# The bias matmul of a graph layer: 128 rows of the array in place of 6

## The chip, the cores and the metric

The kernel runs on one NeuronCore of a Trainium2 chip. A core has a matrix engine (TensorE, in the profile PE, with its weight loads shown apart as PEld), a vector engine (VectorE, DVE), a scalar engine (ScalarE, ACT), GpSimd (POOL) and SyncE (SP), which here only issues transfers. Each engine runs its own instructions in order, and semaphores hold the order between engines. Data come from main memory through 16 DMA engines into the on-chip memory of 128 partitions; TensorE writes its results to a second, smaller memory, PSUM.

The metric is the device time of one launch in microseconds: the median of three runs.

## What is computed

Input x has 32 batches of 512 x 1024 fp32 values, adj is a 512 x 512 matrix. Two layers follow each other, each with a residual and a normalisation over the last axis:

```python
# layer 0: attention over the 1024 nodes
q = einsum('c,bcn->bn', wq, x);  k = einsum('c,bcn->bn', wk, x)
scores = leaky(q[:, None, :] + k[:, :, None])        # slope 0.01
att = softmax(scores, axis=-1)
agg = einsum('bcn,bmn->bcm', x, att)
x = layernorm(x + relu(einsum('oc,bcm->bom', adj, agg) + bm[None, :, None]))
# layer 1
W = adj * adj
x = layernorm(x + einsum('bnf,nm->bmf', x, W) + bias)
```

The bias of layer 1 has 1024 values, one for each column; every row of the 512 x 1024 result of a batch gets the same bias row added. This addition is what the change touches.

## The kernel before, in words

One core works through the 32 batches, several of them in flight at once. A batch passes these stages; the short names are those of the program's functions.

- `load` brings x in (four transfers of 512 KB). `parts` makes the two score vectors on TensorE, with stationary operands of 32 columns (line 220); `cols`, `row_out` and `row` turn and spread them.
- `product` multiplies x by adj, 32 fp32 matmuls a batch (line 311), `product_copy` takes them out of PSUM on ScalarE.
- The softmax isn't formed. The nodes are ranked by score (`rank` on VectorE, `count` on ScalarE), their rows scattered to memory in that order by GpSimd (`scatter`, line 325), loaded back (`sums_load`), summed from both ends (`up`, `down`, and the `carry` matmuls of line 381), and written as a table (`table_write`). For each node `gather` (line 433, GpSimd) fetches the row at its place, and `mix_scale` and `mix` (lines 455 and 460) weigh its two halves.
- `turn` transposes the mixed rows on TensorE (line 484), `residual` adds bm, applies relu and adds x on VectorE (line 492), `spread0`, `root0` and `norm0` normalise.
- Layer 1 is a 512 x 512 by 512 x 1024 product, done in the Winograd form of a 2 x 2 block product with seven smaller products. VectorE forms T1 to T4 from the quarters of x; TensorE runs U, V, Y, C11, Z, C12 and C21 for each of two row groups g. Several of these accumulate in the same PSUM tile: U, V, Y and C21 in `sum_ps`, C11, Z and C12 in `pair_ps`. `quarter` (line 537) runs one such product: two fp32 matmuls of 128 x 128 by 128 x 512, each of which the profile shows as two records.
- ScalarE and VectorE put the parts together (`U_copy`, `V_copy`, `Z_copy`, `upper`, `lower_left`, `lower_right`), `spread1`, `root1` and `norm1` normalise, `store` writes out.

The bias enters inside `quarter`. U starts the `sum_ps` tile, Z starts its half of the `pair_ps` tile, and each does so with one more matmul ahead of the fp32 ones: line 540, `matmul(ps, first, bias_p, start=True, stop=False)`. `bias_p` is the moving operand, 6 rows of 512 bf16 values: each half of the bias row as a sum of three bf16 parts, so that nearly all of fp32 is kept, with signs and sums such that one set of rows serves both U and Z. `first` is the stationary operand, a column of 6 values repeated 128 times by a step of zero: `first_0` for U, `first_10` (all ones) for Z. There are 2 x 2 bias matmuls a batch, 128 in all. Both operands are made once, in `bias_parts` (line 177), which runs in the head of the program, on VectorE.

All work is put in order by hand: a long list of words such as `U.-8.0 ct.-5.4 rk.-5.5` names function, batch (relative) and index, one list for the head, one for the steady loop and one for the tail. `emit` (line 659) calls the functions in that order. Each engine runs its own instructions in the order in which they were emitted. In the steady loop the order on TensorE is, for a batch: transposes, the score matmuls of a later batch, transposes, products, carry, products, U, C11, Z, V, Y, C12, C21, products, carry.

Buffers that matter: x has four buffers, so the load of a batch starts when the C12 matmuls of the batch four before are over; the gathered rows (`got`), the table (`tab`) and the products (`zt`) have one each. PSUM has four half-size tiles (products, scores, carry, `sum_ps`) and two full-size tiles (transposes and `pair_ps`).

Of the kernel before, what the change touches and what calls it, by code (L numbers as in the profile page):

```python
# [35 lines left out]
BF16 = mybir.dt.bfloat16  # L36
# [6 lines left out]
P = 128  # L43
# [6 lines left out]
def adj_resnorm_kernel(  # L50
# [10 lines left out]
    nc = tc.nc  # L61
# [3 lines left out]
    H = 512  # L65
# [4 lines left out]
    const = ctx.enter_context(tc.tile_pool(name="const", bufs=1))  # L70
# [30 lines left out]
    own, spare = small[0:6, 9:14], small[0:1, 14:15]  # L101
# [44 lines left out]
    A11, A12 = adj_2[:, 0:2, 0:Q], adj_2[:, 2:4, 0:Q]  # L146
    S1, minus_A22 = adj_2[:, 0:2, Q:C], adj_2[:, 2:4, Q:C]
    S2, S3, S4 = [const.tile([P, 2, Q], F32, name=f"S{i}") for i in (2, 3, 4)]
    bias_p = const.tile([6, H], BF16, name="bias_p")
    first = const.tile([6, 16], BF16, name="first")  # L150
    first_0, first_10 = first[:, 0:1].broadcast_to([6, P]), first[:, 1:2].broadcast_to([6, P])

    def weights():
        t = p1.tile([P, C], F32, tag="m", name="rows_tp")[:, 0 : 3 * CT]
# [22 lines left out]
    def bias_parts(b):  # L177


        i6 = ident[0:6, 0:6]  # L180
        nc.vector.tensor_tensor(own[:, 0:3], i6[:, 0:3], i6[:, 3:6], ALU.subtract)
        nc.vector.tensor_reduce(own[:, 3:4], i6[:, 3:6], axis=AX.X, op=ALU.add)
        nc.vector.tensor_scalar(own[:, 4:5], own[:, 3:4], -1.0, None, ALU.mult)
        nc.vector.tensor_copy(first[:, 0:1], own[:, 4:5])
        nc.vector.memset(first[:, 1:2], 1.0)
        rest, done = room[:, 0, :], room[:, 1, :]
        for i in range(3):
            part = one.tile([P, H], BF16, tag="junk_s", name=f"bias_part_{i}")[0:6, :]
            nc.vector.tensor_copy(part, rest)
            if i < 2:  # L190
                nc.vector.tensor_tensor(rest, rest, part, ALU.subtract)
            if i == 0:
                nc.vector.tensor_scalar(done, part, own[:, 0:1], None, ALU.mult)
            else:
                nc.vector.scalar_tensor_tensor(
                    done, part, own[:, i : i + 1], done, ALU.mult, ALU.add
                )
        nc.vector.tensor_copy(bias_p, done)

    def apart(group, ins):  # L200

# [435 lines left out]
    def store(b, m):  # L637
# [14 lines left out]
        "11": C11, "12": C12, "21": C21, "Uc": U_copy, "Vc": V_copy, "Zc": Z_copy, "up": upper,  # L652
        "lr": lower_right, "ll": lower_left, "ls": lower_sum, "s1": spread1, "r1": root1,
        "n": norm1, "st": store, "bias": bias_parts,
    }
    pool_ops = ("sc", "g", "r1")
# [306 lines left out]
```

## Time and profile before

| | |
|---|---|
| time of the runs, median of 3 (lowest, highest) | 2055.75 us (2049.65, 2059.41) |
| span of the profiled execution, first to last instruction | 2048.6 us |
| TensorE busy | 1978.8 us (97%), 6353 matmul records |
| weight loads busy | 931.7 us (45%) |
| VectorE busy | 1671.6 us (82%) |
| ScalarE busy | 1491.4 us (73%) |
| GpSimd busy | 864.3 us (42%) |
| traffic | 557.93 MB, mean 272 GB/s |
| mean granted TensorE clock | 0.989 |

The profile gives no time of its own for the profiled execution besides its span. The largest groups on TensorE are the products (line 311, 899.8 us in 2048 records), the seven products of layer 1 (lines 542 and 577), and the transposes (line 484, 131.7 us in 1024 records). In a profile line "128*128" is the size of the stationary operand, rows by columns; what follows is the moving operand or, for weight loads, what is loaded. The number before the bar is busy time in microseconds and the mean of one in nanoseconds; after the bar stands the idle time of the engine just before these instructions and what ended it. "issue" means that nothing in the profile was being waited for. Ends of matmuls are modelled, so their durations overlap; starts are read instead.

### The profile page before, as it was taken

To read this page: it belongs to the slowest core of one execution; us is meant where nothing else is said; L and a number is where in the kernel's file an instruction comes from. 1 tells how busy PE (TensorE), PEld (TensorE's weight loads), DVE (VectorE), ACT (ScalarE), POOL (GpSimd) and SP (SyncE) were. 2 spreads that over 40 slices of the span, in tenths; PEclk is the share of its full clock that TensorE was granted. 3 is DMA by queue.
4 is the path that set the end of the run, shared out by engine and by line. 5 is a ranking of instruction groups with operands and counts; after the bars stand their busy time and mean duration, and the time that the engine had idled before them with its cause. 6 is when DMAs were issued, how large, how long until landed. Compare 5 with 4: busy or idle time off the path is not lost. (4 is left out here: it accounts for less than half of the span.)

```text
span 2048.6 us, 21657 instructions
## 1 busy us (share of the span) xinstructions
PE 1978.8 (97%) x6353; PEld 931.7 (45%) x6353; DVE 1671.6 (82%) x2746; ACT 1491.4 (73%) x2560; POOL 864.3 (42%) x1114
## 2 busy tenths in 40 slices
PE   8999899999999999999999999999999999999876
PEld 4444444444444444444444444444444444444332
DVE  7888887889788888888889888889888888788673
ACT  3567777788677778777777877777877777777566
POOL 5334542544444443443343444343443454444431
PEclk9999999999999999999999999999999999999998
DMA  6758667867678767677867777866777866677752
GB/s 220 283 204 335 257 271 294 314 258 282 237 281 326 297 261 286 268 282 305 313 259 282 274 281 295 323 256 272 283 275 295 329 260 256 247 287 285 273 206 82
DMA packets 142830, 557.93 MB, mean 272 GB/s; under 512 B 15044, under 2 KB 15184, under 8 KB 134520
## 3 DMA queue, kind: packets, MB, share of 16 engines
q1 hardware_dynamic: 85328, 354.38, 44.5%
q0 software_dynamic: 57344, 202.15, 25.6%
q8 instruction: 50, 0.82, 0.2%
q14 instruction: 68, 0.56, 0.1%
q10 hardware_dynamic: 40, 0.02, 0.0%
HBM read 287.07 MB, written 269.42 MB: 272 GB/s over the span
## 5 line engine op out<-in xcount | busy, mean ns | idle before, releaser
L311 PE MATMUL z_ps<-adj_t,x 128*128 128x512 f32 x2048 | 899.8, 593 | 0.0
L311 PEld LDWEIGHTS z_ps<-adj_t,x 128*128 128x128 f32 x2048 | 386.3, 190 | 459.9 <-issue 451.6
L325 POOL DMA_INDIRECT sorted_z<-zt,to x256 | 354.7, 1386 | 450.6 <-ACT zt L317 379.1
L433 POOL DMA_INDIRECT got<-table,of x256 | 278.7, 1089 | 227.1 <-issue 77.7
L272 DVE SCALAR_TENSOR_TENSOR junk_v<-qb,qkc,tie 128x1024 uint8<-128x1024 f32 x256 | 327.9, 1281 | 4.1
L285 ACT ACTIVATE junk_s<-qb,qkc 128x1024 uint8<-128x1024 f32 x256 | 294.4, 1150 | 11.4 <-DVE of L292 5.4
L477 POOL TENSOR_SCALAR tv<-tv 128x1 f32<-128x1 f32 x128 | 41.9, 328 | 469.7 <-ACT junk L470 466.4
L455 ACT ACTIVATE got<-got,w 128x512 f32<-128x512 f32 x256 | 173.2, 714 | 71.6 <-DVE w L450 70.4
L317 ACT COPY zt<-z_ps 128x512 f32<-128x512 f32 x256 | 145.4, 579 | 76.8 <-PE z_ps L311 76.5
L460 DVE SCALAR_TENSOR_TENSOR got<-got,w 128x512 f32<-128x512 f32 x256 | 184.1, 745 | 6.4 <-ACT got L455 5.4
L492 DVE SCALAR_TENSOR_TENSOR x<-agg_ps,small,x 128x1024 f32<-128x1024 f32 x128 | 161.6, 1280 | 18.4 <-PE agg_ps L484 18.0
L373 DVE SCALAR_TENSOR_TENSOR tab<-tab,ac 128x513 f32<-128x513 f32 x224 | 167.7, 748 | 2.1
L597 DVE SCALAR_TENSOR_TENSOR g<-pair_ps,g 128x1024 f32<-128x1024 f32 x64 | 78.2, 1221 | 106.3 <-PE pair_ps L542 100.6
L633 ACT ACTIVATE g<-g,nb,tv 128x1024 f32<-128x1024 f32 x128 | 157.6, 1238 | 5.8 <-POOL nb L627 5.8
L470 ACT ACTIVATE junk<-g,tv 128x1024 uint8<-128x1024 f32 x128 | 146.7, 1146 | 20.7 <-DVE g L597 18.0
L470 ACT ACTIVATE junk<-x,tv 128x1024 uint8<-128x1024 f32 x128 | 147.1, 1149 | 15.6 <-DVE x L492 12.8
L406 DVE TENSOR_TENSOR tab<-tab,carry 128x2052 f32<-128x2052 f32 x64 | 145.0, 2292 | 7.3 <-ACT carry L388 6.6
L363 DVE SCALAR_TENSOR_TENSOR tab<-tab,ac 128x514 f32<-128x514 f32 x192 | 144.1, 750 | 7.4 <-ACT ac L349 5.9
L542 PE MATMUL sum_ps<-x,adj 128*128 128x512 f32 x256 | 130.2, 632 | 16.2 <-ACT x L510 16.2
L484 PE MATMUL agg_ps<-ident,got 128*128 128x128 f32 x1024 | 131.7, 279 | 8.9 <-DVE got L460 3.7
L510 ACT ACTIVATE x<-x,tv 128x1024 f32<-128x1024 f32 x128 | 138.3, 1148 | 1.7 <-DVE tv L506 1.7
L484 PEld LDWEIGHTS agg_ps<-ident,got 128*128 128x128 f32 x1024 | 115.9, 143 | 35.2 <-issue 11.6
(118 smaller groups left out, 2597.7 us busy)
## 6 DMA issues: line engine op xcount, KB each, us to landing
table<-tab SPq DMA_DIRECT2D x64, 2056.0 KB
tab<-sorted_z SPq DMA_DIRECT2D x64, 1028.0 KB
x<-in_x_dram SPq DMA_DIRECT2D x128, 512.0 KB
out_dram<-g SPq DMA_DIRECT2D x128, 512.0 KB
qb<-q_row SPq DMA_DIRECT2D x32, 512.0 KB
sorted_z<-zt,to POOLq DMA_INDIRECT x256, 3.7
got<-table,of POOLq DMA_INDIRECT x256, 8.6
adj_in<-in_adj_dram SPq DMA_DIRECT2D x1, 1024.0 KB
```

Source lines behind the costliest of these rows:

```text
L272: nc.vector.scalar_tensor_tensor(junk, s.qb, s.q[:, j : j + 1], tie[:, at : at + N], ALU.subtract, ALU.is_gt, accum_out=s.rank[:, j : j + 1],)
L285: nc.scalar.activation(junk, s.qb, AF.Sign, bias=s.k[:, j : j + 1], accum_out=s.sign[:, j : j + 1])
L311: nc.tensor.matmul(s.z[j], xt[:, c, j * P : (j + 1) * P], adj_t[:, c, :], start=(c == 0), stop=(c == CT - 1),)
L325: nc.gpsimd.indirect_dma_start(out=sorted_z[b % 2][:, :], out_offset=bass.IndirectOffsetOnAxis(ap=s.to[:, j : j + 1], axis=0), in_=zt[:, j ...
L373: nc.vector.scalar_tensor_tensor(v, v, c, s.zs[:, j + 1, 0:D], ALU.mult, ALU.add)
L433: nc.gpsimd.indirect_dma_start(out=s.got[:, j, :], out_offset=None, in_=table[b % 2][:, :], in_offset=bass.IndirectOffsetOnAxis(ap=s.of[:, ...
L455: nc.scalar.activation(down, down, AF.Copy, scale=s.w[:, 1, j : j + 1])
L460: nc.vector.scalar_tensor_tensor(up, up, s.w[:, 0, j : j + 1], down, ALU.mult, ALU.add)
L470: nc.scalar.activation(junk, t, AF.Square, bias=v[0][:, i : i + 1], scale=-float(N), accum_out=v[1][:, i : i + 1],)
L484: nc.tensor.transpose(s.agg[o][:, j * P : (j + 1) * P], s.got[:, j, o * P : (o + 1) * P], ident)
L492: nc.vector.scalar_tensor_tensor(t[:, o, :], s.agg[o], nbm[:, o : o + 1], t[:, o, :], ALU.max, ALU.add, accum_out=s.v0[0][:, o : o + 1],)
L633: nc.scalar.activation(g, g, AF.Identity, bias=s.nb[:, m : m + 1], scale=s.v1[1][:, m : m + 1])
```

## The change

The two operands of the bias matmul get 128 rows. Both tiles are set to zero once, and the six rows of values are then written into rows 0 to 5 as before. The matmul on line 540 keeps its text; its operands are now 128 x 128 and 128 x 512 in place of 6 x 128 and 6 x 512. The added rows contribute zeros to the sum.

```diff
-    bias_p = const.tile([6, H], BF16, name="bias_p")
-    first = const.tile([6, 16], BF16, name="first")
-    first_0, first_10 = first[:, 0:1].broadcast_to([6, P]), first[:, 1:2].broadcast_to([6, P])
+    bias_p = const.tile([P, H], BF16, name="bias_p")
+    first = const.tile([P, 16], BF16, name="first")
+    first_0, first_10 = first[:, 0:1].broadcast_to([P, P]), first[:, 1:2].broadcast_to([P, P])
+    nc.vector.memset(bias_p, 0.0)
+    nc.vector.memset(first, 0.0)
...
-        nc.vector.tensor_copy(first[:, 0:1], own[:, 4:5])
-        nc.vector.memset(first[:, 1:2], 1.0)
+        nc.vector.tensor_copy(first[0:6, 0:1], own[:, 4:5])
+        nc.vector.memset(first[0:6, 1:2], 1.0)
...
-        nc.vector.tensor_copy(bias_p, done)
+        nc.vector.tensor_copy(bias_p[0:6, :], done)
```

## The prediction

> **What bounds the kernel now.** I read the page's busy shares first, then busy time by stretch, then the groups of the changed line with shapes kept apart, and last the order in time around one bias matmul.
>
> Busy time by stretch (first the length, then the time and count of each engine, the granted clock, the DMA share, GB/s):
>
> ```profile
> 740.00:1040.00 300.00, 300.00 (x972) 141.60 (x972) 252.69 (x418) 227.75 (x394) 125.40 (x167) 1.00 0.73 286
> 1040.00:1340.00 300.00, 300.00 (x933) 140.65 (x932) 252.79 (x418) 227.69 (x391) 126.55 (x165) 1.00 0.74 287
> ...
> 1900.00:2048.60 148.60, 108.92 (x307) 48.68 (x305) 80.28 (x128) 90.43 (x140) 45.76 (x71) 0.91 0.51 193
> ```
>
> In the middle TensorE (first engine column) has no idle microsecond, at full clock; VectorE has 16% free, ScalarE 24%. So a microsecond taken from TensorE there is a microsecond of the kernel until another chain comes due. In the last 149 us TensorE idles 40.
>
> The changed line, by form (busy us, mean ns | idle before it):
>
> ```profile
> L540 PE MATMUL sum_ps<-bias_p,first 6*128 6x512 bf16 x64 | 24.6, 385 | 1.1 <-ACT zt L317 1.1
> L540 PE MATMUL pair_ps<-bias_p,first 6*128 6x512 bf16 x64 | 24.6, 385 | 0.0
> L540 PEld LDWEIGHTS <-first 6*128 6x128 bf16 x128 | 11.7, 91 | 96.7 <-issue 96.7
> ```
>
> The 385 ns has a modelled end and is no price. The telling figure is the last: the weight path stands idle 96.7 / 128 = 0.76 us before each load of `first`, with nothing to wait for. Before an ordinary load it is 0.24 us.
>
> Matmuls in order of time (start, us, ...), then weight loads:
>
> ```profile
> 1002.24 0.38 PE L540 MATMUL pair_ps<-bias_p,first 6*128 6x512 bf16 x1
> 1002.55 1.98 PE L542 MATMUL pair_ps<-x,adj 128*128 128x512 f32 x4
> 1004.47 0.38 PE L540 MATMUL pair_ps<-bias_p,first 6*128 6x512 bf16 x1
> ...
> 1010.04 1.88 PE L542 MATMUL sum_ps<-zt,S 128*128 128x512 f32 x4
> 1011.75 1.88 PE L542 MATMUL pair_ps<-x,S 128*128 128x512 f32 x4
> 1013.47 1.88 PE L542 MATMUL sum_ps<-zt,S 128*128 128x512 f32 x4
> ```
>
> ```profile
> 1001.28 0.19 PEld L577 LDWEIGHTS pair_ps<-x,adj 128*128 128x128 f32 x1 [0.24 <-issue]
> 1002.23 0.09 PEld L540 LDWEIGHTS <-first 6*128 6x128 bf16 x1 [0.76 <-issue]
> 1002.55 0.30 PEld L542 LDWEIGHTS pair_ps<-x,adj 128*128 128x128 f32 x2 [0.23 <-DVE junk_v L272]
> ```
>
> Four fp32 records take 1013.47 - 1011.75 = 1.72 us (1.715 over several), and each holds two passes of 512 columns: 0.214 us a pass. With a bias matmul ahead, the same four take 1004.47 - 1002.24 = 2.23 us. So one bias matmul costs 0.515 us, although it is one pass of 512 columns: **0.30 us of it is bubble**. An ordinary load starts while the matmul before runs, so the matmul follows at once. The load of `first` starts at 1002.23, 0.09 after the last fp32 pass streamed out (1001.71 + 0.43), and its matmul starts with it; the next fp32 load again starts only after the bias matmul. 0.09 pause + 0.09 load + 0.215 pass + 0.02 + 0.11 load = 0.52: both loads around it are exposed.
>
> [...] The trace agrees as far as it can: it has one other change of tile, fp32 to fp32 with no change of type, the 32-column matmuls of the scores, with the same mark before and an exposed load after:
>
> ```profile
> 62.94 0.19 PEld L311 LDWEIGHTS z_ps<-adj_t,x 128*128 128x128 f32 x1 [0.24 <-issue]
> 63.89 1.45 PEld L220 LDWEIGHTS qk_ps<-x,wqk 128*32 128x32 f32 x32 [0.76 <-issue]
> 65.76 0.73 PEld L381 LDWEIGHTS carry_ps_True<-end,before 128*128 128x128 f32 x4 [0.41 <-issue]
> ```
>
> Again 0.76. From plain matmuls to transposes, full tile to full tile, there is no gap (carry at 1034.07, four records of 0.215, transposes at 1034.94). What the trace lacks is bf16 on a full tile: whether the type alone breaks the overlap isn't shown. [...] here 6 rows took 91 ns and an exposed 128-row load 0.11 us, near enough.
>
> **The change, part by part.**
>
> Two memsets. 512 bf16 columns at the rate of the `tie` memset (1.66 us for 1920) are 0.44 us, 16 columns 0.06 as the small memsets. They stand on VectorE after the `zero` memset (ends 3.91), ahead of the copy at 7.20, which waits 3.29 us for TensorE. Cost 0; without that cover, 0.5 us once. Nothing else waits on them: the first bias matmul is at 133.3. The two copies and the small memset into rows 0 to 5 have their old sizes: 0. SyncE and GpSimd get nothing new.
>
> The 128 matmuls: one pass of 512 columns stays, on 128 rows. Lower bound of its cost: fully overlapped, 0.214, a saving of 0.30 each, at most 38.5 us in all. Nothing lets it go lower. Upper bound: the bubble stays and the load takes 0.19 (the duration of overlapped 128-row fp32 loads) in place of 0.09: 0.10 worse each. I take full overlap, because an exposed load comes with a change of tile everywhere I looked and never without one.
>
> Where the saving counts (bias matmuls by stretch): 3 before 140 us, 18 in 140 to 440, 95 in 440 to 1900, 9 in 1900 to 2007, 3 after. The chain of waits runs from 1896 to 2008 outside TensorE (sorting, table, gathers, mixing, residual); TensorE even waits 11.6 us for ScalarE at 1971. So those 9 count nothing; the last 3 are on the chain. 119 x 0.301 = 35.8 us.
>
> Deductions. In 140 to 440 TensorE waits 14.8 us in all (4.6 and 3.2 for ScalarE's copy, 2.6 for a T3, smaller ones), released partly by things that don't move with it. I let 8 of the 18 fall into those: 2.4 us.
>
> In the steady loop (61.06 us a batch) the U pair of bias matmuls comes ahead of the copies that release the last scatters; from there, scatter, eight gathers, their landing, and mixing run beside TensorE to the transposes, and the Z pair lies alongside. So the U pair's 0.6 us moves both paths, the Z pair's 0.6 us only TensorE's. How much room is there? Mixing against transposes, an ordinary batch and a tight one:
>
> ```profile
> 1092.75 2.21 DVE L460 SCALAR_TENSOR_TENSOR got<-got,w 128x512 f32<-128x512 f32 x3
> 1096.18 1.91 PE L484 MATMUL agg_ps<-ident,got 128*128 128x128 f32 x16
> ```
>
> ```profile
> 1032.94 2.21 DVE L460 SCALAR_TENSOR_TENSOR got<-got,w 128x512 f32<-128x512 f32 x3
> 1034.94 1.91 PE L484 MATMUL agg_ps<-ident,got 128*128 128x128 f32 x16
> ```
>
> The last mix serves the fourth transpose, 0.33 us after the first: room 1.55 us in the ordinary batch, 0.12 in the tight one. Of eight batches from 668 to 1096 two are tight, six have 1.4 to 2.0. One batch in five, say, of some 25, loses 0.5 us: 2.5 us. Next late after that is the gathers' landing, since the load of x starts when C12 ends, so earlier, and shares the DMA engines (74% busy) with them; the ordinary batch has 1 us left for it. Between transposes and U no bias matmul lies, so the norm that U waits for (ends 1053.83, U at 1055.57) isn't pressed.
>
> Sum: 35.8 - 2.4 - 2.5 = **30.9 us saved**. The profiled span of 2048.6 becomes 2017.7. For that execution only its span is given; the median of the runs lies 7.15 above it, the lowest 1.05. I keep that distance: 2055.75 - 30.9 = **2025 us**.
>
> **The rivals.**
>
> The type, not the tile, breaks the overlap: fp32 to bf16 and back costs what it costs on any number of rows. For it: every bias matmul changes both at once. Against: the 0.76 mark of the scores, where the type stays. Time 2056, no change. Chance 0.12.
>
> Half: one of the two exposed loads is cured, say that of `first`, not the fp32 one after. About half of 31: 2040. Chance 0.07.
>
> Slower: the bubble stays for the type's sake and the load, in the open ahead of each bias matmul, takes 0.19 over 128 rows where 6 took 0.09. 119 x 0.10 = 11.9 us: 2068. It passes 0.5% from 0.086 us a matmul (10.3 / 119). Against: the exposed 128-row load at 1002.55 took 0.11 before its matmul. Chance 0.05.
>
> That the matmul stays a small tile (trailing zeros cut away) is excluded: it is given 128 rows, and the score matmuls' tile follows their operand's width.
>
> **How the numbers follow.** Full overlap 0.76, with a range of its own: 2013 (all 38.5 and the runs' spread of 4) to 2037 (12 more microseconds lost to gathers and ties). The half case reaches to 2047. Together these leave out the no-change and slower cases, 0.17, and a few hundredths of edge: 2013 to 2047. 0.5% (10.3 us) is about what a measurement of this kernel can tell from no change. Faster 0.76 + 0.07 = 0.83, same 0.12, slower 0.05.
>
> **What would show it.** Right: bias matmul shown as 128*128, idle before its load near 0.24 us, start of bias matmul to start of the next 1.93 us in place of 2.23, batch period near 60 us, and short waits of transposes on VectorE's mix in the tight batches. Wrong: 0.76 still there with 128*128 (the type did it); 2.23 gone but the period still 61 (the gathers have taken over).

## The result, and the profile after

The changed kernel takes 2054.66 us (median of 20 runs, 2049.41 to 2062.92) beside 2054.91 for the kernel before (20 runs, 2047.89 to 2059.41): ratio 1.0004, 95% interval 0.9994 to 1.0013. The change does nothing to the time that can be measured; 31 us fewer were forecast. The profiled execution has a span of 2048.0 us beside 2048.6.

And yet the change did on TensorE just what it was to do. The line of the bias matmul by form, in the changed kernel (its line numbers are 2 higher than before; the kernels of the experiments have their own):

```profile
L542 PE MATMUL pair_ps<-bias_p,first 128*128 128x512 bf16 x60 | 22.7, 379 | 0.0
L542 PEld LDWEIGHTS <-first 128*128 128x128 bf16 x128 | 12.6, 99 | 30.5 <-issue 30.5
```

The idle time of the weight path before a load of `first` is 30.5 / 128 = 0.24 us in place of 0.76, the mark of an ordinary load. (60 records in place of 64: some matmul records are missing from this trace.) The same stretch of one batch, in order of time:

```profile
1000.79 0.38 PE L542 MATMUL pair_ps<-bias_p,first 128*128 128x512 bf16 x1
1001.00 1.88 PE L544 MATMUL pair_ps<-x,adj 128*128 128x512 f32 x4
1002.72 0.38 PE L542 MATMUL pair_ps<-bias_p,first 128*128 128x512 bf16 x1
```

From bias matmul to bias matmul it is 1002.72 - 1000.79 = 1.93 us in place of 2.23: the bubble of 0.30 is gone, all of it. To the start of the next matmul the bias matmul now takes 0.21 us, half of the 0.43 us of an fp32 record ((1002.72 - 1001.00) / 4), so that a record counts as two such passes, as in the forecast. TensorE's own work of a batch falls from 61.03 us to 61.03 - 4 x 0.30 = 59.83. But now TensorE has idle time in the middle, where it had none, in the view by stretch:

```profile
740.00:1040.00 300.00, 298.41 (x976) 143.97 (x980) 253.51 (x419) 229.54 (x396) 128.16 (x167) 1.00 0.74 287
1040.00:1340.00 300.00, 297.85 (x951) 143.60 (x958) 254.22 (x420) 230.18 (x396) 128.82 (x167) 1.00 0.74 287
```

The first column after the length is TensorE: 298.41 and 297.85 of 300 where before both stretches were full. (Since ends of matmuls are modelled, small lags inside a run of matmuls still show as busy, so the loss is larger than these 2 us.) In the view of waits TensorE waits for one thing in the loop (740 to 1640 us), and VectorE is held up longer than before by the landing of the gathered rows. Engine and line, what it waited for, us in total, times, longest; first the changed kernel's TensorE and VectorE:

```profile
PE carry_ps_True L383 <- ACT zt L319: 5.4, 8, 1.3
...
DVE w L448 <- DMA got<-table,of: 70.0, 30, 3.7
```

then VectorE in the kernel before, where TensorE had no wait at all in these 900 us:

```profile
DVE w L446 <- DMA got<-table,of: 43.6, 24, 3.2
```

VectorE waits 70 us in place of 44 for the landing, in 30 batch halves in place of 24; its wait for TensorE fell meanwhile (line 599, 56.1 us, for 74.0). What TensorE gained reappears as a wait for a transfer.

Where in the program the time is given back, read from the starts of the score matmuls (us from the span's start):

| | score matmul of batch 8 | batch 25 | batch 31 | end of span |
|---|---|---|---|---|
| before | 420.5 | 1464.6 | 1834.4 | 2048.6 |
| changed | 423.7 | 1462.4 | 1833.9 | 2048.0 |

From batch 8 to 25, 17 periods, 17 x 1.20 = 20.4 us could be had; 1044.1 - 1038.7 = 5.4 came. The mean period of batches 10 to 23 is 60.81 us beside 61.09; single batches of the changed kernel have 60.0 to 61.8. Ahead of that, between batches 7 and 8, the changed kernel has one period of 68.9 us where it was 63.1, and near the end, between batches 28 and 29, one of 66.6 where it was 61.9. (The score matmuls run three batches ahead of layer 1, so the first is the passage of layer 1 from batch 4 to 5.) These two places alone cost 10.5 us, more than the gain of the loop; the period after the second of them gives 1.2 back (57.2 for 58.4).

The granted clock is no cause in the loop: there it is 1.00 in both kernels, and a kernel below with a mean clock of 0.985, beside 0.984 for the changed one, is 29 us faster. At the passage from batch 4 to 5 it has a part. After a wait of 6.64 us four matmul records of C21 run at half clock and take 3.58 us, where the kernel before, at full clock, takes 1.82 (the changed kernel first; the third number from the end is the clock):

```profile
401.82:405.40 3.58, 3.58 (x5) 1.52 (x5) 3.48 (x10) 0.00 (x0) 0.00 (x0) 0.50 1.04 412
```

```profile
400.54:402.36 1.82, 1.82 (x4) 0.86 (x5) 1.82 (x4) 0.00 (x0) 0.00 (x0) 1.00 1.04 407
```

That is 1.8 us of the 5.8 lost there. From 1900 us to the end the mean clock is 0.88 beside 0.91; what this costs is not separated.

**The second loop.** Followed from batch to batch, the work outside the bias matmuls forms a ring of its own: carry matmuls, transposes, scores, products, the carry downwards, its copy on ScalarE, the table's last sums on VectorE, ranks and T1 to T3, the gathers on GpSimd, their landing, the weights of the mixing, the mixing on ScalarE, with product copies queued behind it, and with them a free PSUM tile for the next carry. The chain of waits of the changed kernel shows it (start, length, engine, what):

```profile
804.94 0.38 ACT carry L390
...
820.97 1.98 POOL got L435
...
831.08 13.20 DMA got<-table,of
...
850.53 0.48 ACT zt L319
851.05 0.70 PE carry_ps_True L383 x2
```

In this turn of the ring, from one carry to the next, the landing is the longest piece, 13.20 us. No bias matmul lies on this ring. How the end of it looks in one batch (its U starts at 993.49), in order of time on all engines:

```profile
1026.93 0.17 DVE L448 TENSOR_TENSOR w<-bd,got 128x8 f32<-128x8 f32 x1 [3.16 <-DMA got<-table,of]
...
1027.75 0.72 ACT L457 ACTIVATE got<-got,w 128x512 f32<-128x512 f32 x1 [1.77 <-DVE w L452]
...
1032.96 1.53 ACT L319 COPY zt<-z_ps 128x512 f32<-128x512 f32 x3
1033.58 0.70 PE L383 MATMUL carry_ps_True<-end,before 128*128 128x257 f32 x2 [0.86 <-ACT zt L319]
```

The last gathered rows land 33.4 us after U (read, here and below, from the start of their weighing on VectorE). ScalarE has waited 1.77 us for the weights; its last mixing ends at 1033.06, the product copies stand behind it, and the second half of the carry waits 0.86 us for them. The carry of the same batch in the kernel before runs without a gap:

```profile
1034.07 1.03 PE L381 MATMUL carry_ps_True<-end,before 128*128 128x257 f32 x4
```

In 12 of batches 10 to 23 the changed kernel starts the second half of the carry 0.05 us after such a copy ends, so the copy holds it; in the kernel before this is so in one.

**Why the landing is late.** The load of x (2.1 MB) starts as soon as the C12 matmuls have ended, and so moves with TensorE: 22.80 us after U before, 21.70 now (medians of batches 10 to 23). The first gather, though, starts 9.27 us after U before and 9.36 now. So the load moved 1.1 us into the gathers. From 15 us after U to the landing of the gathered rows, with the sorted rows, the gathered ones and x under way, the DMA share stays above 1. The kernel before, by stretches of 3 us (U at 1055.57; the last two columns are the DMA share and GB/s):

```profile
1070.57:1073.57 3.00, 3.00 (x9) 1.32 (x8) 0.00 (x0) 3.00 (x7) 2.22 (x3) 1.00 1.03 409
...
1085.57:1088.57 3.00, 3.00 (x9) 1.33 (x8) 1.07 (x7) 1.54 (x3) 2.01 (x6) 1.00 1.02 408
1088.57:1091.57 3.00, 3.00 (x9) 1.33 (x8) 3.00 (x7) 3.00 (x6) 0.32 (x1) 1.00 0.18 70
```

For six such stretches in a row the rate is 400 to 414 GB/s at a share of 1.02 to 1.04; in the next 3 us it is 70, and after that nothing is moved. The mean share of 0.74 over 300 us hides this. (The view counts a packet's bytes and time where it starts, so that a share can pass 1, and single stretches elsewhere read higher, 443 GB/s at 1.05 from 1058.57 us; what the engines could move at most, no run shows.) That the stretch is full is the author's estimate from its share. If it is full, x can only come earlier at the cost of the gathered rows: their last landing moved from 31.95 to 32.80 us after U, 0.85 later, while TensorE's carry is due 1.10 us earlier (38.63 us after U for 39.73). That the one comes of the other is for the experiments to show.

### The profile page after: what moved, and what is told of

It reads as the page before. It is cut to its first block, busy times and chain, and to the rows that moved or that the text cites. A ratio compares the mean times of both kernels' runs of the same rounds, so it can differ in the third digit from the quotient of the medians.

```text
span 2048.0 us, 21627 instructions
## 1 busy us (share of the span) xinstructions
PE 1956.9 (96%) x6321; PEld 945.1 (46%) x6353; DVE 1670.9 (82%) x2748; ACT 1491.8 (73%) x2560; POOL 874.5 (43%) x1114
## 4 chain that ended last, share of the span: by engine, by line
PE 45%; DMA 16%; DVE 11%; POOL 8%; ACT 5%; issue 5%; SPq 0%; DVEq 0%; ACTq 0%; POOLq 0%
PE z_ps L313 20%; DMA got<-table,of 12%; PE sum_ps L544 9%; POOL got L435 6%; PE agg_ps L486 4%; PE pair_ps L544 4%; DVE tab L408 3%; DVE junk_v L274 3%; PE pair_ps L579 3%; PE qk_ps L222 2%; DMA sorted_z<-zt,to 2%; ACT junk L472 2%; POOL sorted_z L327 1%; DVE got L462 1%; ACT got L457 1%
## 5 line engine op out<-in xcount | busy, mean ns | idle before, releaser
L327 POOL DMA_INDIRECT sorted_z<-zt,to x256 | 367.6, 1436 | 436.1 <-ACT zt L319 367.8
L479 POOL TENSOR_SCALAR tv<-tv 128x1 f32<-128x1 f32 x128 | 46.7, 365 | 470.1 <-ACT junk L472 466.8
## 6 DMA issues: line engine op xcount, KB each, us to landing
table<-tab SPq DMA_DIRECT2D x64, 2056.0 KB
```

The source lines that it names most:

```text
L327: nc.gpsimd.indirect_dma_start(out=sorted_z[b % 2][:, :], out_offset=bass.IndirectOffsetOnAxis(ap=s.to[:, j : j + 1], axis=0), in_=zt[:, j ...
```

## The experiments

Two theories stood against each other. The ring: the loop is held by the carry, gather and mixing ring at about the period that TensorE had, and what holds the ring is the x load's collision with the gathers. The rival: TensorE still sets the period, and the saving goes astray elsewhere, in the head, the tail or the clock. Each kernel was timed 5 to 22 times beside the kernel before, in five groups on five chips; the kernel before had a median of 2056.0 us beside the first four, 2055.5 beside no bias with the load held and the full hold with the other order, 2054.2 and 2054.3 beside the two holds behind half, 2051.6 beside the last. So kernels of different groups are compared by their ratios.

### No bias matmul at all

```diff
-        if first is not None:
-            nc.tensor.matmul(ps, first, bias_p, start=True, stop=False)
...
-                ps, a[:, k, g * P : (g + 1) * P], v[:, k, :], start=False, stop=(k == 1),
+                ps, a[:, k, g * P : (g + 1) * P], v[:, k, :],
+                start=(first is not None and k == 0), stop=(k == 1),
```

This leaves out the addition of the bias, from the kernel before.

> The kernel before with line 540 taken out and the first fp32 matmul of U and Z starting the sum: the addition of the layer-1 bias is left out. TensorE has 128 x 0.515 = 66 us less to do than before, 27 us less than the changed kernel. Second-loop theory (the loop transposes, table, T3, gathers, landing, mixing, transposes takes 60 to 61.5 us a batch and holds no bias matmul): steady batch period stays at 60.0 to 61.0, time 2045 to 2058. Rival (TensorE is still what bounds, and the 38 us of the change were lost to something the padded rows cost elsewhere): 119 x 0.515 off, about 1994.

Measured 2054.19 us, ratio 0.9992 (0.9977 to 1.0006). All 128 matmuls gone, and no time gone. TensorE's wait for a carry in the loop (740 to 1640 us):

```profile
PE carry_ps_True L381 <- ACT zt L317: 22.5, 14, 2.8
```

The mean period is 61.53 us, longer than before and than expected, and the rows land 33.0 us after U, with the load earlier still (20.83). In all of batches 10 to 23 the second half of the carry starts 0.05 us after a product copy ends. In three of them the clock also falls to 0.50 for 3.4 us after the wait (its mean is 0.99 in each 300 us from 740 to 1640 us). The ring holds the loop; TensorE's saving, of whatever size, is returned at the carry. This already settles that the forecast did not fail over the bubble.

### The load of x held back, on 128 rows and on 6

A 4-byte transfer on SyncE reads the last weights of the mixing, and the load of the batch three ahead stands behind it in SyncE's order. It then starts when all gathered rows have landed. (The first three lines are in `parts`: a load still held when its x is needed goes out there.)

```diff
+        if b in late:
+            late.discard(b)
+            load(b)
...
+    def load_word(b):
+        if b < 6:
+            load(b)
+        else:
+            late.add(b)
+
+    def load_behind(b):
+        nc.sync.dma_start(out=mark, in_=st[b].w[0:1, 1, NT - 1 : NT])
+        late.discard(b + 3)
+        load(b + 3)
...
+        if h == 1 and b + 3 in late:
+            load_behind(b)
...
-        "ld": load, "pa": parts, ...
+        "ld": load_word, "pa": parts, ...
```

The changed kernel with it:

> The changed kernel with the load of x held back until the last gathered rows of that batch have been weighed, from batch 6 on (a 4-byte transfer that reads the weights goes ahead of it on SyncE's queue). The 2 MB of x leave the stretch in which the gathers land. Second-loop theory: second landing 4 to 5 us earlier after U, steady period down to TensorE's own 59.83, no long waits near 400 and 1700 us; time 2028 to 2042. Rival (the saving is lost on TensorE itself, to half-clock stretches or waits unrelated to the gathers): period stays near 60.6, time 2050 to 2058.

The kernel before with it:

> The same hold of the x load in the kernel before (6 rows). Second-loop theory: here TensorE sets the steady period, so it stays at 61.03 although the rows land 4 to 5 us earlier; only the tight batches gain: 2046 to 2055. If the late load is worth something by itself whatever the bias matmul costs: as much gained as with 128 rows, 2030 to 2042.

Measured, on 128 rows: 2025.38 us (2024.5 to 2026.84), ratio 0.9844 (0.9831 to 0.9856). On 6 rows: 2051.78 us, ratio 0.9977 (0.9964 to 0.9990). One stretch of the loop, on 128 rows:

```profile
740.00:1040.00 300.00, 300.00 (x992) 146.53 (x991) 259.16 (x427) 233.11 (x401) 136.07 (x171) 1.00 0.76 290
```

TensorE is full again, at a period of 59.83 us, its own work to the hundredth; on 6 rows the period is 61.03. With the hold the change is worth 2051.78 - 2025.38 = 26.4 us; without it, nothing. The hold alone is worth 4 us, since TensorE then sets the period. Neither edit shows its worth without the other. In the loop the hold moves the load alone: what SyncE issues next, a store of the result, starts 41.6 us after U in one batch of either kernel with 128 rows (1096.46 - 1054.84 without the hold, 1085.51 - 1043.88 with it). Two things were expected otherwise: the rows land 2.7 and 2.2 us earlier, not 4 to 5, and on 128 rows the long wait near 400 us stays (a period of 70.8 us there, where the held kernel on 6 rows has 63.1); the time is nevertheless 3 us below the expected range.

In the changed kernel without and with the hold, TensorE runs each batch alike, to 0.01 us, from U to the carry, which starts 38.63 us after U in both. The transposes then start at 39.50 us in every batch with the hold, and at 39.50 to 41.10 (mean 40.12) without. The whole excess of the period, 0.98 us, arises between the carry and the turned scores, 6.4 us further on with the hold.

### T1 to T4 ahead of the rank passes

If not the transfer but the start of the gathers on GpSimd held the ring, an earlier and shorter first gather would shorten it. The words of the loop, and of four batches of the tail:

```diff
-... rc.0 tw.-2.1 U.-3.0 ... Uc.-3.1 t1.-3 Uc.-3.0 ... t2.-3 ... t3.-3 g.-2.2 t4.-3
+... rc.0 t1.-3 t2.-3 t3.-3 t4.-3 tw.-2.1 U.-3.0 ... Uc.-3.1 Uc.-3.0 ... g.-2.2
```

In one late batch the moved T4 comes ahead of a product copy that shares part of its tile, so that this batch's values differ; the instructions are the same.

> The changed kernel with T1 to T4 moved ahead of four rank passes on VectorE, in the loop and four batches of the tail. They then no longer run beside the last scatters and the first gather, which take 1.9 and 2.0 us there against 1.0 elsewhere. Second-loop theory: gathers done 1.5 to 2 us earlier after U, steady period 59.9 to 60.3, time 2040 to 2049. Rival (saving lost on TensorE itself): 2050 to 2058.

Measured 2055.38 us, ratio 0.9997 (0.9982 to 1.0012): a miss. The first gather took 1.05 us in most batches in place of 1.98 and the last one ended 0.7 us earlier (19.72 after U, not 20.41), but the rows landed only 0.45 earlier (32.35), and the period stayed at 60.72. Ending the issue 0.7 us earlier moved the landing by less, and the period hardly at all; moving the load of x, above and below, moves both.

### No bias matmul and the load held back

Is 59.83 with the hold TensorE's figure, or by chance the ring's? Without the bias matmuls TensorE's own work is 58.97 us.

> The bias addition is left out (no bias matmul at all), and the load of x is held behind the weighing of the last gathered rows from batch 6 on. Left-out bias alone gave 2054.2 us at a period of 61.5, so TensorE was far from the bound. Theory (the second loop carry, transposes, sorting, gathers, mixing is close to TensorE's 61 us, and the collision of the x load with the gathers is what holds it there): with the load out of the way the period falls towards TensorE's own 61.03 - 4 x 0.515 = 58.97 us, and the time to 2000 to 2012 us. Rival A (the second loop is bound at about 59.8 us by its own chain, whatever the load of x does, and the held changed kernel stands at 59.83 for that reason and not for TensorE's): period 59.5 to 60, 2020 to 2030 us, with TensorE waiting 1 us a batch at the carry. Rival B (the load of x has nothing to do with it here): 2050 to 2056.

Measured 2002.83 us (2001.12 to 2004.9), ratio 0.9749 (0.9732 to 0.9767), period 58.97:

```profile
740.00:1040.00 300.00, 300.00 (x984) 146.71 (x983) 262.73 (x432) 236.76 (x407) 138.48 (x174) 1.00 0.77 296
```

Full again. With the load out of the way the ring would bear even a shorter TensorE. The same removal of the bias that gave nothing now gives 0.9977 - 0.9749 = 2.3%, some 47 us, against the kernel on 6 rows with the hold.

### The load held behind half of the rows

How much of the load has to be out of the way? The hold was put behind the weighing of the first four of the eight gathers, in two ways.

```diff
-        nc.sync.dma_start(out=mark, in_=st[b].w[0:1, 1, NT - 1 : NT])
+        nc.sync.dma_start(out=mark, in_=st[b].w[0:1, 1, NT // 2 - 1 : NT // 2])
...
-        if h == 1 and b + 3 in late:
+        if h == 0 and b + 3 in late:
```

> The changed kernel with the load of x held behind the weighing of the first half of the gathered rows (about 25 us after the start of U) in place of the second half (31.3), from batch 6 on. The load's start and the last landing so far: at 21.7 the rows had landed at 32.8 (period 60.81), at 31.3 at 30.1 (period 59.83). Theory (what the load of x moves ahead of the last landing is what delays it, byte for byte): the load starts some 3.5 us later than in the changed kernel, so the landing comes between the two, 31 to 32, and the period at 59.85 to 60.3; time 2025 to 2040 us. Rival (holding the load helps through something else, such as the order on the DMA queue or the copies around it, and any hold does as much): landing 30, 2025 us and period 59.83 at once. Other rival (only a load wholly behind the landing helps): landing 32.8, 2050 to 2056.

Measured 2084.05 us, ratio 1.0138 (1.0115 to 1.0161), slower than all others, and no test of the question: in the order by hand the load's word comes after the weighing of the first half, so the hold found nothing to hold, and the load fell back to where `parts` needs it. In the loop it started 21.70 us after U, as without a hold; in some batches of the head and tail only 37 to 50 us after, and the score matmuls waited 22.4 us in all for x. With the hold also taken when the word comes later:

```diff
         if b < 6:
             load(b)
-        else:
+        elif st[b - 3].w is None:
             late.add(b)
+        else:
+            load_behind(b - 3)
```

> The changed kernel with the load of x held behind the weighing of the first half of the gathered rows, now also where the load's word comes after that weighing in the order; in the run before this one the hold took hold in no ordinary batch, and the load still started at 21.7 us after U. The load should now start near 25 to 26 us. The load's start and the last landing so far: 21.7 and 32.8 (period 60.81), 31.3 and 30.1 (period 59.83). Theory (what the load of x moves ahead of the last landing is what delays it, byte for byte): the landing comes between the two, 31 to 32, period 59.85 to 60.3, time 2025 to 2040 us. Rival (holding the load helps through something else, and any hold does as much): landing 30, period 59.83, 2025 us. Other rival (only a load wholly behind the landing helps): landing 32.8, 2050 us or more.

Measured 2020.33 us (2017.66 to 2020.55), ratio 0.9834 (0.9812 to 0.9856), below the expected range. SyncE in one batch (U at 1045.47), the small transfer and then the load:

```profile
1069.56 0.24 SPq L455 DMA_DIRECT2D mark<-w  x1
1069.91 1.83 SPq L87 DMA_DIRECT2D x<-in_x_dram  x4
```

and the weighing of both halves on VectorE, with the wait for the landing in brackets:

```profile
1068.75 0.17 DVE L467 TENSOR_TENSOR w<-bd,got 128x8 f32<-128x8 f32 x1 [1.35 <-DMA got<-table,of]
...
1075.90 0.17 DVE L467 TENSOR_TENSOR w<-bd,got 128x8 f32<-128x8 f32 x1 [1.11 <-DMA got<-table,of]
```

Medians of batches 10 to 23, in us after U:

| kernel | first gather | load of x starts | last rows landed | first transpose | mean period |
|---|---|---|---|---|---|
| before | 9.27 | 22.80 | 31.95 | 40.60 | 61.09 |
| changed | 9.36 | 21.70 | 32.80 | 39.98 | 60.81 |
| changed, held behind half | 9.36 | 24.58 | 30.99 | 39.50 | 59.89 |
| changed, held behind all | 9.37 | 31.30 | 30.14 | 39.50 | 59.84 |
| before, held behind all | 9.27 | 30.94 | 29.78 | 40.60 | 61.03 |
| no bias | 9.16 | 20.83 | 33.00 | 40.18 | 61.53 |
| no bias, held behind all | 8.90 | 30.77 | 29.61 | 38.64 | 58.97 |

In all seven the gathers start within 0.5 us of one another and the issue of the last one ends at 20.3 to 20.6; what moves is the load of x, and the landing follows it: from the changed kernel to the hold behind half, 2.9 us later for the load is 1.8 earlier for the landing. The rival that any hold does as much falls for the landing (30.99 is not 30.14), and so does the one that only a load wholly behind helps. The collision is shown: the landing goes with the start of the load, in its order and by most of its size, while the gathers stand still. In the loop both holds leave TensorE the bound (59.89 and 59.84 us), so that they differ by little. Their ratios, 0.9834 and 0.9844, don't differ clear of noise; in the traces the hold behind half gains at the end, where the last three periods of the score matmuls are 59.8, 57.2 and 60.9 us for 63.4, 60.6 and 62.3.

### The passage from batch 4 to 5, and both together

In the changed kernel C21 of batch 4 waits long for VectorE. TensorE, in order of time:

```profile
401.82 3.78 PE L544 MATMUL sum_ps<-zt,adj 128*128 128x512 f32 x4 [6.64 <-DVE g L605]
```

VectorE, for its part, stands in front of the sums over a later batch's sorted rows, with C21's combining (line 605) queued behind:

```profile
400.67 0.49 DVE L360 TENSOR_SCALAR tab<-tab,ac 128x514 f32<-128x514 f32 x1 [9.26 <-ACT ac L351]
401.07 0.68 DVE L605 SCALAR_TENSOR_TENSOR g<-sum_ps,g 128x512 f32<-128x512 f32 x1
```

ScalarE's `ac` waits 8.47 us for the sorted rows to land. On the changed kernel with the full hold, the order of the head was edited at this place:

```diff
-... u.6.0 g.5.6 12.4.0 lr.4.0 u.6.1 g.5.5 up.4.1 21.4.0 g.5.4 lr.4.1 ...
+... g.5.6 12.4.0 lr.4.0 g.5.5 up.4.1 21.4.0 g.5.4 lr.4.1 u.6.0 u.6.1 ...
```

> The changed kernel with the load of x held behind the weighing of the last gathered rows, and in the order of the head two products of batch 6 (u.6.0, u.6.1) put behind the combining of batch 4's C21, so that VectorE's combining isn't queued behind a wait for the exponentials of sorted rows that landed late. Theory (the place from batch 4 to 5 where the changed kernel lost 5.8 us is a wait of VectorE in its own order, the second place after the loop): TensorE's wait of some 6.6 us at C21 near 400 us falls below 2, time 2018 to 2022 us against 2025.4 of the held changed kernel. Rival (the lateness there comes from the landing itself and only moves to the next instruction that needs it): 2024 to 2028.

Measured 2019.97 us (2015.21 to 2027.43), ratio 0.9840 (0.9815 to 0.9865). The wait is gone (TensorE's waits for that combining are 1.8 us in all) and the period there fell from 70.8 to 64.6 us, but the runs spread over 12 us, and against the 2025.38 of the kernel without this edit the time alone proves nothing. VectorE now ends the combining at 396.2 and waits 5.67 us for the same sums after it, and the clock from 395 to 412 us is 1.00 in place of 0.80; from 380 to 430 us TensorE has three waits left, of 1.4 us at most.

Both edits together, the hold behind half and this order:

> Both edits together: the load of x held behind the weighing of the first half of the gathered rows, and two products of batch 6 put behind the combining of batch 4's C21 in the order of the head. Theory (the two losses lie at different places, the loop and the passage from batch 4 to 5, so they add): 2012 to 2017 us, no wait of TensorE over 3 us at C21 near 400 us, period 59.83. Rival (the gain of the half hold over the full one, 5 us, and that of the reordering, 5 us, are the same microseconds): 2019 to 2022.

Measured 2013.56 us (2012.0 to 2014.11), ratio 0.9816 (0.9803 to 0.9829): 1.8% faster than the kernel before, and the lowest ratio of those with the bias kept. Its interval overlaps that of the hold behind half alone, so the time doesn't show that the gains add. The traces, one execution each, speak for it: the passage falls from 70.9 to 64.6 us, as it does with the full hold (70.8 to 64.6), and the last three periods stay at 59.8, 57.2 and 60.9.

## Why the prediction was wrong, step by step

- **The bubble: right, in kind and in size; its cause was not shown.** 0.30 us a matmul, the mark of 0.76 us, and both are gone with 128 rows: 1.93 us, 0.24 us. The type of the operands changes as before, so the type was not the cause. That a change of tile stands behind the number of rows was the author's estimate, from the same 0.76 us at the score matmuls; no run tells the two apart. The rival "type, not tile" gave the right time, 2056, for a reason that the trace refutes; "half" and the slower one, with a load left in the open, are refuted by the same lines.
- **Memsets at nothing: right.** They take 0.27 and 0.07 us, not 0.44 and 0.06, at 3.9 to 4.1 us, inside the wait that was named.
- **119 bubbles on the path, 35.8 us: right only where TensorE bounds.** In the loop of the held kernels each of the four counts in full, 61.03 to 59.83 us a batch; over the launch 26.4 us come; in the traces the passage from batch 4 to 5 takes 7.7 us more with 128 rows.
- **The deduction of 2.5 us for the loop: this is the step that failed.** It says that the U pair "moves both paths", that the ordinary batch has 1.55 us of room at the transposes, and "1 us left" after the Z pair. The room of 1.55 us was read rightly (batches 10 to 23 have 1.40 in the median). Two terms were not. First, the U pair moved nothing on the other path: the first scatter did start 0.5 us earlier after U (5.91 for 6.41), but it took 1.89 us in place of 1.29, and the first gather starts in both kernels when T3 ends on VectorE, whose order runs from pass to pass without a gap: 9.36 us after U for 9.27. So the room shrinks by all that TensorE comes earlier to the carry, 1.10 us relative to U, and not by the Z pair's 0.6 alone. Second, the collision of the load with the gathers was named as "next late" and priced at nothing: it moves the landing 0.85 us later. What comes due first is also a step ahead of the transposes, at the second half of the carry, behind ScalarE's product copies. There the kernel before had 1.56 us of room in the median batch; 1.56 - 1.10 - 0.85 = -0.39, and it starts 0.39 us late in the median batch (39.45 for 39.06 with the hold). The first transpose follows 0.62 us late in the mean (40.12 for 39.50), and the two runs of transposes behind it take some 0.2 us more each in a late batch, for a reason that no run shows; together 0.98 us a batch of the 1.20.
- **2.4 us off in the head: mis-sized.** The passage from batch 4 to 5 alone gives 5.8 us back. The wait at C21 near 402 us, 6.64 us, was 1.52 before, and the half clock after it takes 1.8; the landing of sorted rows, not only ScalarE's copies, sets the pace there. What makes the 4.7 us between batches 28 and 29 was not taken apart.
- **What would show it wrong was named** ("2.23 gone but the period still 61 (the gathers have taken over)"), but no case of the forecast carried it: the rivals were all about TensorE, and none about the other loop. The fill of the DMA engines was read as the mean, 74%, and not in the window that mattered, where it is 1.02 to 1.04.

## What to carry to other kernels

An engine at 100% shows that it is the bound, not how far the next one is behind: follow the loop that avoids this engine from batch to batch, and compare its length with the period, before multiplying a saving by its count. Ask of every transfer that is released by the faster engine what it will run beside, in the DMA share of that very window and not of the span. A saving that measures as nothing may be whole and waiting: here one small hold on a prefetch that nobody needed yet turned 0 into 26 us, and a hold of a third of that length (the load at 24.6 us, not 31.3) did as well.

## What the runs showed of the hardware

- The bf16 matmul of 128 x 128 by 128 x 512 between fp32 matmuls takes 0.21 us from its start to the next (1000.79 to 1001.00) in the changed kernel, half of an fp32 record's 0.43, and its load, 99 ns in the mean, starts 0.43 us ahead of it (1000.36), so that it is hidden. On 6 rows the same matmul costs 0.515 us (2.23 - 1.715).
- How long a scatter or gather occupies GpSimd goes with what VectorE is doing. The first scatter of a batch takes 1.29 us in the kernel before and 1.89 in the changed one, where it starts 0.5 us earlier and so has more left of a VectorE pass with two inputs in on-chip memory (line 528 there). GpSimd in the changed kernel, in order of time:

```profile
1060.74 1.89 POOL L327 DMA_INDIRECT sorted_z<-zt,to  x1 [8.95 <-ACT zt L319]
...
1064.20 1.98 POOL L435 DMA_INDIRECT got<-table,of  x1 [0.30 <-DVE zt L533]
1066.48 0.96 POOL L435 DMA_INDIRECT got<-table,of  x1 [0.30 <-issue]
```

and VectorE at the same time:

```profile
1060.57 1.22 DVE L528 TENSOR_TENSOR T<-x 128x1024 f32<-128x1024 f32 x1
...
1064.11 1.21 DVE L537 TENSOR_TENSOR zt<-T,x 128x1024 f32<-128x1024 f32 x1
```

  The slow scatter lies beside line 528, the first gather starts when line 533 ends (1064.19) and lies beside line 537. In the kernel before, from 740 to 1640 us, all 121 scatters and gathers that start while such a VectorE instruction has been under way for over 0.1 us end 0.81 to 0.98 us after it, and take 0.97 to 2.40; the 16 beside a VectorE instruction that reads PSUM take 0.94 to 0.96, the 59 beside an idle VectorE 0.93 to 0.95. The changed kernel has 121 of the first kind with the same bounds. Why, no run shows. The rank passes have two such inputs as well: the 31 scatters and gathers beside one (line 272 of the kernel before) are among the 121 and take 1.00 to 1.84 us. In the kernel with T1 to T4 moved the scatter, beside rank passes there, still took 1.91 us.
- Sixteen DMA engines, mostly on sorted rows, gathered rows and blocks of x, held 400 to 414 GB/s, at a share of 1.02 to 1.04, for 18 us in the batch looked at (kernel before, 1070.57 to 1088.57 us).
